# Graph convolution on one core: twelve products of zeros added to every group's open sum of messages

## The chip, the cores and the metric

The kernel runs on one core of one Trainium2 chip. The metric is device time in microseconds (us) of one execution; three runs give a median. The engines are named as the profile names them: PE (TensorE, matrix products, with PEld for its weight loads), DVE (VectorE), ACT (ScalarE), POOL (GpSimd, which here issues the gathers) and SP (SyncE, which issues the other DMAs).

## The reference, cut to what matters

Two graph layers run one after the other over 6250 nodes and 200000 edges that are sorted by destination. The first is a two-layer attention network, the second a convolution with radial weights. The change touches only the convolution:

```python
e0, e1 = f0[edge_src], f1[edge_src]                       # 128 numbers per edge, gathered
h = gelu(gelu(edge_scalar_attr @ W_mlp1 * c1) @ W_mlp2 * c2)
w = einsum('pxu,ex->epu', W_tp, h)                        # 4 x 32 weights per edge
mid = concatenate([w0*e0*a0, w3*(e1.a1), w1*e0*a1, w2*e1*a0])   # 256 numbers per edge
agg = zeros.at[edge_dst].add(mid)                         # sum of messages per node
out = mix of agg @ Wf0, agg @ Wf1 and the node's own part
```

## The kernel before, in words

**Tiles, groups, chunks.** The edges are cut into 1563 tiles of 128, one edge per partition. Eight tiles make a group (196 groups), and three groups, 24 tiles (`CT`), make a chunk. A chunk's messages are added into one sum `whole` in PSUM, 128 node slots by 256 columns, of which there is a single buffer. A Python loop over groups writes the program out in full; `keep` holds the instructions of each engine in the order in which the loop writes them, so that each engine is a queue whose first instruction blocks those behind it.

**One group on each engine.**
- POOL issues eight gathers, one per tile, into a tile `G` (line 353). There are six `G` buffers; a gather waits until ACT and DVE have read the buffer's old contents.
- ACT runs two gelus (`hid`, line 1479), eight scalings of the gathered rows (`g`, line 1495), and in some groups a copy.
- PE runs the two layers of the small network (line 1476: `layer<-a8t` with 16 rows, then `layer<-hid`), eight products for the weights (`big`, line 1488), and eight products that add the messages into the sum (`whole<-mess,ohr`, line 1531). These are fp32, and each stands in the trace as two records.
- DVE multiplies out the messages (lines 1508 to 1517) and makes the next group's one-hot matrix (`ohr`, line 1524).
- SP issues the loads of `a8t` (line 1595) and of what a chunk's end needs.

**The order on PE** decides much below. In all groups it begins with `layer<-a8t` for a later group. In a chunk's first group the eight weight products, `layer<-hid` and the eight message products follow; the first of these opens the new sum, so it needs ACT's copy of the old one (`acc<-whole`, line 1561, in `close`), which stands on ACT between the two `hid`. After six of the eight, two products at line 1579 carry the old sum's shared nodes over. In the second group `layer<-a8t` is followed by the transposes of the old sum (line 1539); in the third, by the chunk's last products (lines 1544 and 1545), whose result ACT copies at line 1547 (`o`). After these come `layer<-hid`, the weight products and the message products, as before.

The first message product of a chunk starts the sum (`k == 0`), and the last one closes it (`k == end` in `sink`).

Of the kernel before, what the change touches and what calls it, by code (L numbers as in the profile page):

```python
# [32 lines left out]
BF16 = mybir.dt.bfloat16  # L33
# [10 lines left out]
P = 128  # L44
# [4 lines left out]
WSTEP = 16  # L49
HS = 7  # L50
CT, LT = 24, 40
DENSE1 = 24
LAG_D, AFTER, AFTER_D = 11, 4, 7
GP, GK, GSB = 125, 16, 4
# [10 lines left out]
def gnn_kernel(ctx: ExitStack, tc: tile.TileContext, x, src, dst, attr4, attr8,  # L65
# [3 lines left out]
    nc = tc.nc  # L69
    N, D = x.shape  # L70
# [23 lines left out]
    NT = src_t.shape[1]  # L94
    NG = NB - DENSE1
    HALF = P // 2
# [16 lines left out]
    keep = tc.keep_in_program_order  # L113

    def big():
        return ps_big.tile([P, 8, P], F32, tag="big", name="big")
# [10 lines left out]
    def whole():  # L127
        return ps_acc.tile([P, 512], F32, tag="acc", name="whole")
# [392 lines left out]
    def flags(pool, *why):  # L521

        flag = pool.tile([1, NB + 1], F32, name="flag")
        nc.vector.tensor_copy(flag[:, :NB], why[0])
        for w in why[1:]:
            nc.vector.tensor_tensor(flag[:, :NB], flag[:, :NB], w, op=OP.max)
        nc.vector.tensor_reduce(flag[:, NB:], flag[:, :NB], axis=AX.X, op=OP.max)
        flag_i = pool.tile([1, NB + 1], I32, name="flag_i")
        nc.vector.tensor_copy(flag_i, flag)
        return flag_i[:, :NB], flag_i[:, NB:]  # L530
# [146 lines left out]
    keep = lambda ins: ins  # L677
# [78 lines left out]
    rhs1 = [dram.tile([P, NB, HW], BF16, name=f"rhs1{q}") for q in range(H1 // 2)]  # L756
    deg1 = pool.tile([P, DENSE1], F32, name="deg1")

# [185 lines left out]
    def miscounted(pool, deg, edges, n):  # L944


        many = pool.tile([P, n], F32, name=f"many{n}")
        nc.vector.tensor_scalar(many, deg, 256.0, None, op0=OP.is_gt)
        ps = small()
        nc.tensor.matmul(ps[:1, :n], ones, deg, start=True, stop=True)  # L950
        nc.tensor.matmul(ps[:1, P:P + n], ones, many, start=True, stop=True)
        miss = pool.tile([1, n], F32, name=f"miss{n}")
        nc.vector.tensor_tensor(miss, ps[:1, :n], edges, op=OP.subtract)
        nc.vector.tensor_tensor(miss, miss, ps[:1, P:P + n], op=OP.subtract)
        nc.vector.tensor_scalar(miss, miss, -0.5, None, op0=OP.is_lt)
        return miss

    HH = H1 // 2 * C1
    assert DENSE1 % 4 == 0
    passes = [(b0, q) for b0 in range(NG, NB, 4) for q in range(H1 // 2)]  # L960
# [173 lines left out]
    def chunk_of(g):  # L1134
        return (g * SB + HT // 2) // HT

    def first_of(c):
        return max(0, HT * c - HT // 2)

    def last_of(c):  # L1140
        return HT * c + HT // 2
# [13 lines left out]
    def scatter(g, tiles):  # L1155
        c = chunk_of(g)
        if tiles[0] == 0 and g * SB == first_of(c):
            kept1["acc"] = whole()[:, :HD + H1]
        for t in tiles:
            nc.tensor.matmul(kept1["acc"], ohs[g][:, t, :], mss[g][:, t],  # L1160
                             start=g * SB + t == first_of(c), stop=g * SB + t + 1 == last_of(c))
# [85 lines left out]
    keep = plain  # L1247
    nc.vector.tensor_scalar(wtp_sb[:, 0:3, :], wtp_sb[:, 0:3, :], 1.0 / math.sqrt(HID), None, op0=OP.mult)
    nc.vector.tensor_scalar(wtp_sb[:, 3, :], wtp_sb[:, 3, :], 1.0 / math.sqrt(3.0 * HID), None, op0=OP.mult)
    written_order.close()  # L1250
    nc.vector.tensor_tensor(over1[:, NG:], over1[:, NG:], miscounted(pool, deg1, n_edges[:, NG:], DENSE1), op=OP.max)
    again, some = flags(pool, over1, wide1.to_broadcast([1, NB]))
# [58 lines left out]
    with tc.tile_pool(name="att2", bufs=1) as pool, tc.tile_pool(name="dense", bufs=2) as dense, \  # L1311
# [68 lines left out]
        for b0 in range(0, NB, 2):  # L1380
            n = min(2, NB - b0)
# [10 lines left out]
            acc = big().rearrange("p (k a) c -> p k (a c)", k=2)  # L1392
            if b0 == 8:
                load_tiles(pool)
            for h0 in range(0, NB, HS):
# [15 lines left out]
                for j, made in ((0, up), (1, down)):  # L1411
                    for h in range(HS):
                        for k in range(n):
                            nc.tensor.matmul(acc[:, k, j * C2:(j + 1) * C2], made[:, h, k * P:(k + 1) * P],
                                             rhs2[:, h0 + h, j, :],
                                             start=h0 + h + j == 0, stop=h0 + h + j == NB)
# [3 lines left out]
            acc = acc[:, :n, :2 * C2].rearrange("p k (j c) -> p k j c", j=2)  # L1420
# [30 lines left out]
    cw = ctx.enter_context(tc.tile_pool(name="cw", bufs=2))  # L1451
# [46 lines left out]
    def messages(G, g0, n, a1, pw, then, between):  # L1498


        w = pw[:, :n, :].rearrange("e c (p u) -> e c p u", p=4)
        ms = cw.tile([P, SB, 2, 4, MUL], F32, name="mess", bufs=3)
        e0 = G[:, :n, :MUL]
        e1 = G[:, :n, MUL:].rearrange("e c (i u) -> e c i u", i=3)
        s4 = [P, n, 3, MUL]

        dot = cw.tile([P, SB, 3, MUL], F32, name="dot", bufs=1)
        keep(nc.vector.tensor_tensor(dot[:, :n], e1, a1[:, :, :, None].to_broadcast(s4), op=OP.mult))  # L1508
        dot1 = cw.tile([P, SB, MUL], F32, name="dot1", bufs=1)
        keep(nc.vector.tensor_reduce(dot1[:, :n], dot[:, :n].rearrange("e c i u -> e c u i"), axis=AX.X, op=OP.add))  # L1510
        w1 = cw.tile([P, SB, MUL], F32, name="w1", bufs=1)
        keep(nc.vector.tensor_tensor(w1[:, :n], w[:, :, 1, :], e0, op=OP.mult))  # L1512
        keep(nc.vector.tensor_tensor(ms[:, :n, 1, 0], w[:, :, 3, :], dot1[:, :n], op=OP.mult))
        keep(nc.vector.tensor_tensor(ms[:, :n, 1, 1:], w[:, :, 2, :][:, :, None, :].to_broadcast(s4),
                                     g0[:, :n, MUL:].rearrange("e c (i u) -> e c i u", i=3), op=OP.mult))
        keep(nc.vector.tensor_tensor(ms[:, :n, 0, 0], w[:, :, 0, :], g0[:, :n, :MUL], op=OP.mult))  # L1516
        keep(nc.vector.tensor_tensor(ms[:, :n, 0, 1:], w1[:, :n, None, :].to_broadcast(s4),  # L1517
                                     a1[:, :, :, None].to_broadcast(s4), op=OP.mult))
        between()
        got = then and then()  # L1520
        return ms, got

    def one_hot3(dl, n, oh):
        keep(nc.vector.tensor_tensor(oh[:, :n, :], slot[:, None, :].to_broadcast([P, n, P]),  # L1524
                          dl[:, :, None].to_broadcast([P, n, P]), op=OP.is_equal))
        return oh

    def scatter(ms, oh, cs, sink):
        for c in cs:
            acc, start, stop = sink(c)  # L1530
            keep(nc.tensor.matmul(acc, oh[:, c, :], ms[:, c].rearrange("e h i u -> e (h i u)"), start=start, stop=stop))  # L1531
# [19 lines left out]
    with tc.tile_pool(name="conv", bufs=1) as pool, tc.tile_pool(name="gath3", bufs=6) as gath:  # L1551
# [4 lines left out]
        state, todo = {}, deque()  # L1556
# [12 lines left out]
        def sink(t):  # L1569
            c, k = divmod(t, CT)  # L1570
            end = min(CT, NT - c * CT) - 1
            if k == 0:
                state["acc"] = whole()[:, :2 * D]
            if k == min(6, end) and c:

                same = cw.tile([P, P], F32, name="same")
                keep(nc.vector.tensor_scalar(same, slot, shift[:, c - 1:c], None, op0=OP.is_equal))
                for a in state["sums"]:
                    keep(nc.tensor.matmul(state["acc"], same, a, start=False, stop=False))  # L1579
            return state["acc"], k == 0, k == end  # L1580

        groups = [(t, min(SB, NT - t)) for t in range(0, NT, SB)]

        def hots(g):
            t, n = groups[g]
            return one_hot3(dstc[:, t:t + n], n, cw.tile([P, SB, P], F32, name="ohr", bufs=3))

        def layers(g):
            if g >= len(groups):
                return iter(())  # L1590
            t, n = groups[g]
            a8t = cw.tile([2 * NRAD, NPR * P], F32, name="a8t", bufs=4)
            for j in range(2 if n > NPR else 1):
                c = (t + j * NPR) * P
                nc.sync.dma_start(a8t[j * NRAD:(j + 1) * NRAD, :], attr8_t[:, c:c + NPR * P])
            return hidden(n, a8t)
# [8 lines left out]
        def keep_a1(t):  # L1605
            m = min(LT, NT - t)
            a1s = kept[:, P + t // LT % 2 * 3 * LT:P + (t // LT % 2 + 1) * 3 * LT].rearrange("p (k f) -> p k f", f=3)
            keep(nc.vector.tensor_copy(a1s[:, :m], a4s[t][:, :m, 1:]))
            return a1s
# [21 lines left out]
        for g, (t, n) in enumerate(groups):  # L1631
            G, g0 = rows
            i = t % LT
            last = g + 1 == len(groups)
            ms, after = messages(G, g0, n, a1s[:, i:i + n, :], pws.popleft(), None if last else lambda: hots(g + 1),
                                 lambda: hids.extend(list(second)[-1:]))
            if i + SB == LT and t + SB < NT:
                a1s = keep_a1(t + SB)
            first = layers(g + 3)
            next(first, None)  # L1640
            if not last:
                rows = fetch(g + 1)
            next(first, None)
            pw = big() if hids or todo else None
            if todo:
                todo.popleft().send(pw)
                next(first, None)
            if t and t % CT == 0:
                close(t // CT - 1)
            if hids:  # L1650
                pws.append(weigh(groups[g + 2][1], hids.popleft(), pw))
            next(first, None)
            scatter(ms, oh, range(n), lambda c: sink(t + c))
            second = first
            oh = after
# [117 lines left out]
```

## Time and profile before

| What | Value |
|---|---|
| median of 3 runs | 4942.67 us (4939.53 to 4945.52) |
| profiled execution | 4904.63 us, span 4902.8 us |
| mean granted PE clock | 0.796 of full speed |
| convolution, 2400 to 4800 us of the span: PE, DVE, ACT, POOL busy | 1599.58, 1105.17, 684.29, 1374.04 us |
| the same stretch: granted PE clock, share of DMA engines | 0.78, 0.18 |

The span is the time from the first to the last instruction of one profiled execution. Busy time is the union of an engine's instructions. A row of the timeline gives start, length, engine, line, operation, tiles, shapes and count; in brackets stands how long the engine was idle before and what ended that. "remote" means that a semaphore did so and that the profile found no instruction that ended just then.

### The profile page before, as it was taken

The page shows a single profiled execution, that of the slowest core. Times are in us where ns is not written, and L with a number is a line of the kernel's source. Part 1 is how long each engine was busy: PE and PEld are TensorE (multiplying, and loading weights), DVE is VectorE, ACT ScalarE, POOL GpSimd, SP SyncE. Part 2 cuts the span into 40 slices and gives each one's busy share as a digit, 9 for nine tenths or more (in the row PEclk, how much of TensorE's full clock was granted, in tenths as well). Part 3 has the DMA queues.
Part 4 walks back from the last instruction along what each step waited for, and adds up shares of the span by engine and source line. Part 5 has one row for each costly group of instructions (what it writes and reads, how often), then busy time and mean ns, then how long its engine had stood idle before and what let it go on. Part 6 is the DMA issues. An engine that isn't in the chain of part 4 may idle for free.

```text
span 4902.8 us, 63767 instructions
## 1 busy us (share of the span) xinstructions
PE 3315.7 (68%) x21302; PEld 2434.5 (50%) x21303; DVE 2951.3 (60%) x4901; ACT 2432.3 (50%) x5811; POOL 2488.7 (51%) x2440
## 2 busy tenths in 40 slices
PE   3247777777667789995466766666666675666667
PEld 3145555555445578884244444444444443444445
DVE  5458778788778779995344444444444444444445
ACT  3238878888678679995223322222222232222233
POOL 4556666667556500002555555555555555555553
PEclk6558878889788789997677877777777877777788
DMA  3346666667566554442111111111111111111111
GB/s 100 91 119 180 176 173 178 176 184 198 155 166 185 165 217 158 166 171 74 46 45 48 48 48 47 47 48 47 47 49 47 47 49 47 46 48 48 47 46 30
DMA packets 420348, 491.23 MB, mean 100 GB/s; under 512 B 267937, under 2 KB 303628, under 8 KB 419998
## 3 DMA queue, kind: packets, MB, share of 16 engines
q1 hardware_dynamic: 340900, 345.68, 23.4%
q0 software_dynamic: 78304, 139.36, 11.8%
q8 instruction: 175, 2.87, 0.2%
q10 hardware_dynamic: 794, 1.88, 0.1%
q14 instruction: 175, 1.43, 0.1%
HBM read 383.20 MB, written 103.42 MB: 99 GB/s over the span
## 4 chain that ended last, share of the span: by engine, by line
another core or an unknown queue 21%; PE 19%; ACT 6%; issue 5%; DVE 2%; DMA 0%; DVEq 0%; ACTq 0%; SPq 0%
PE whole L1531 9%; PE layer L1476 6%; ACT g L1495 4%; PE big L1488 3%; ACT hid L1479 1%; DVE mess L1517 1%; PE whole L1579 0%; PE big L1544 0%; DVE ohr L1524 0%; DVE dot L1508 0%; DVE mess L1516 0%; DMA G<-table,srcc 0%; DVE dot L1510 0%; PE big L1539 0%
## 5 line engine op out<-in xcount | busy, mean ns | idle before, releaser
L353 POOL DMA_INDIRECT G<-table,srcc x1563 | 1475.1, 944 | 1622.4 <-ACT g L1495 571.8
L353 POOL DMA_INDIRECT G<-table,srcw x808 | 955.1, 1182 | 616.9 <-DVE msg L394 294.4
L1479 ACT ACTIVATE hid<-layer 128x512 f32<-128x512 f32 x392 | 233.5, 596 | 1605.2 <-remote 963.2
L1531 PE MATMUL whole<-mess,ohr 128*128 128x256 f32 x3126 | 819.4, 417 | 0.5 <-ACT acc L1561 0.5
L1096 ACT ACTIVATE up<-erb,sel 128x512 bf16<-128x512 f32 x1176 | 809.3, 739 | 0.4 <-PE small L878 0.4
L1476 PE MATMUL layer<-hid,wm_sb 128*128 128x512 f32 x392 | 301.4, 860 | 676.8 <-ACT hid L1479 464.9
L1531 PEld LDWEIGHTS whole<-mess,ohr 128*128 128x128 f32 x3126 | 649.9, 212 | 157.1 <-issue 53.3
L878 PE MATMUL small<-key,lo 128*128 128x98 bf16 x3136 | 315.0, 232 | 387.9 <-ACT ca L860 165.4
L860 ACT CAST ca<-small 128x392 bf16<-128x392 f32 x784 | 385.7, 495 | 291.2 <-remote 135.6
L878 PEld LDWEIGHTS <-lo 128*128 128x128 bf16 x3136 | 285.0, 123 | 478.3 <-issue 447.5
L1524 DVE TENSOR_TENSOR ohr<-kept,dstc 128x1024 f32<-128x1024 f32 x196 | 238.6, 1218 | 470.4 <-remote 337.7
L1512 DVE TENSOR_TENSOR w<-big,G 128x256 f32<-128x256 f32 x196 | 82.5, 421 | 696.4 <-PE big L1488 308.8
L1011 PE MATMUL up<-up,rc 128*102 128x512 bf16 x1176 | 475.3, 437 | 37.8 <-DVE up L1020 11.7
L1495 ACT ACTIVATE g<-G,a 128x128 f32<-128x128 f32 x1563 | 475.4, 390 | 0.0
L1401 ACT ACTIVATE ramp<-erb,sel 128x256 bf16<-128x256 f32 (+1 forms) x1138 | 458.0, 493 | 13.4 <-DVE up L1409 7.5
L1488 PEld LDWEIGHTS big<-wtp_sb,hid 64*128 64x128 f32 x3126 | 258.3, 246 | 386.0 <-ACT o L1547 211.0
L1476 PEld LDWEIGHTS layer<-hid,wm_sb 128*128 128x128 f32 x392 | 74.1, 237 | 714.4 <-ACT hid L1479 487.0
L1488 PE MATMUL big<-wtp_sb,hid 64*128 64x128 f32 x3126 | 303.7, 349 | 180.8 <-ACT o L1547 151.1
L1020 DVE TENSOR_TENSOR up<-up,ctc 128x3584 bf16<-128x3584 bf16 x168 | 339.4, 2020 | 55.1 <-ACT up L1096 26.5
L1160 PEld LDWEIGHTS whole<-msg,ohr 128*128 128x128 f32 x1616 | 329.5, 242 | 61.7 <-issue 21.2
L852 DVE TENSOR_TENSOR lo<-slots,turned 128x2048 bf16<-128x2048 bf16 x196 | 238.5, 1217 | 155.2 <-PE small L878 87.5
L1160 PE MATMUL whole<-msg,ohr 128*128 128x68 f32 x1616 | 322.6, 315 | 0.7 <-ACT ring L1166 0.7
(316 smaller groups left out, 5100.3 us busy)
## 6 DMA issues: line engine op xcount, KB each, us to landing
counts<-ca SPq DMA_DIRECT2D x196, 392.0 KB
ct<-counts SPq DMA_DIRECT2D x196, 392.0 KB
ctc<-counts SPq DMA_DIRECT2D x1344, 56.0 KB
rc<-rhs SPq DMA_DIRECT2D x84, 358.8 KB
oht<-dlow SPq DMA_DIRECT2D x50, 512.0 KB
G<-table,srcc POOLq DMA_INDIRECT x1563
G<-table,srcw POOLq DMA_INDIRECT x808
a8t<-attr_rows SPq DMA_DIRECT2D x391, 16.0 KB
```

The costliest lines, as they stand in the source:

```text
L353: nc.gpsimd.indirect_dma_start(out=G[:, c, :], out_offset=None, in_=table, in_offset=bass.IndirectOffsetOnAxis(ap=idx[:, c:c + 1], axis=0))
L860: nc.scalar.copy(ca[:, :, k * W:(k + WBANK) * W].rearrange("p h (k d) -> p h k d", d=W), ps[:, :WBANK * NKEY].rearrange("p (k h d) -> p h ...
L878: nc.tensor.matmul(ps[:, n * NKEY:(n + 1) * NKEY], lo[:, a, :, r], ky[:, a, :, r], start=True, stop=True)
L1011: nc.tensor.matmul(sums["ups"][j][:2 * C1, :], r[:, i, c:c + 2 * C1], up[:, i], start=h0 + i == 0, stop=h0 + i == NB - 1)
L1020: nc.vector.tensor_tensor(by_part, by_part, state["ct", p, h0].rearrange("p k a h d -> p h (k a) d"), op=OP.min)
L1096: nc.scalar.activation(up[:, i], state["erb", p][:, j], AF.Relu, bias=sel1[:, h0 + i, 2 * q + j:2 * q + j + 1], scale=STEEP)
L1160: nc.tensor.matmul(kept1["acc"], ohs[g][:, t, :], mss[g][:, t], start=g * SB + t == first_of(c), stop=g * SB + t + 1 == last_of(c))
L1401: nc.scalar.activation(ramp[:, h, :n * P], erb[:, :n * P], AF.Relu, bias=sel2[:, h0 + h, :], scale=STEEP)
L1476: keep(nc.tensor.matmul(ph, w, x[:, :npr * P], start=True, stop=True))
L1488: keep(nc.tensor.matmul(pw[:, c, :], hid[half, j * P:(j + 1) * P], wtp_sb[half].rearrange("x p u -> x (p u)"), start=True, stop=True))
L1495: keep(nc.scalar.activation(g0[:, c], G[:, c, :], AF.Copy, scale=a0[:, c, :]))
L1531: keep(nc.tensor.matmul(acc, oh[:, c, :], ms[:, c].rearrange("e h i u -> e (h i u)"), start=start, stop=stop))
```

## The change

A tile of 128 by 128 bf16 zeros is made once. In every group but the first, right after `layer<-a8t` on PE, twelve products of this tile with 256 columns of zeros (one column, read 256 times) are added into the sum `whole` that is then open. In a chunk's first group this is still the old chunk's sum, and the last of the twelve closes it; the message products no longer do, save the very last. The values of the sum stay what they were.

```diff
+BUSY = 12
...
+    nothing = cw.tile([P, P], BF16, name="nothing", bufs=1)
+    nc.vector.memset(nothing, 0.0)
+
+    def busy(acc, n, stop):
+
+        for i in range(n):
+            keep(nc.tensor.matmul(acc, nothing, nothing[:, 0:1].to_broadcast([P, 2 * D]),
+                                  start=False, stop=stop and i == n - 1))
+
...
-            return state["acc"], k == 0, k == end
+            return state["acc"], k == 0, t + 1 == NT
...
             next(first, None)
+            if t:
+                busy(state["acc"], BUSY, t % CT == 0)
             pw = big() if hids or todo else None
```

In the built program this is 2340 products, each with a weight load of its own (195 groups times 12), and one memset on DVE. All other instructions stand in their old order on every engine. One wait is new: ACT's copy `acc<-whole` now waits for the last of the twelve products before it; before the change its data were known to be there from the wait of the `hid` ahead of it.

## The prediction

> **What bounds the kernel now.** I read the page first, for the stages.
>
> ```profile
> PE 3315.7 (68%) x21302; PEld 2434.5 (50%) x21303; DVE 2951.3 (60%) x4901; ACT 2432.3 (50%) x5811; POOL 2488.7 (51%) x2440
> ...
> POOL 4556666667556500002555555555555555555553
> PEclk6558878889788789997677877777777877777788
> ...
> L353 POOL DMA_INDIRECT G<-table,srcc x1563 | 1475.1, 944 | 1622.4 <-ACT g L1495 571.8
> ```
>
> No engine is full. From slice 20 on, the convolution, POOL is busy five tenths and the granted clock is 0.7 to 0.8. The busy times by stretch and the waits of line 353 tell more (the second is "idle until: us, times").
>
> ```profile
> 2400.00:4800.00 2400.00, 1599.58 (x7268) 1071.81 (x7267) 1105.17 (x1549) 684.29 (x2002) 1374.04 (x1456) 0.78 0.18 47
> ```
>
> ```profile
>   ACT g L1495: 548.6, 98
> ```
>
> In these 2400 us POOL issues 1456 gathers, so 182 groups, so a chunk of three groups takes 2400 / (182 / 3) = 39.6 us. A gather costs 0.944 us and 0.30 us of issue; 24 of them make 29.9 us. The other 9.7 us of a chunk POOL stands idle, nearly always for ACT's `g`. So the chunk lasts as long as POOL's gathers plus POOL's waits, and the question is what makes ACT late. The timeline of one chunk shows it.
>
> ```profile
> 3056.01 1.12 PE L1476 MATMUL layer<-a8t,wm_sb 16*128 16x512 f32 x2
> ...
> 3065.69 0.60 ACT L1479 ACTIVATE hid<-layer 128x512 f32<-128x512 f32 x1 [11.39 <-remote]
> 3066.34 2.08 PE L1476 MATMUL layer<-hid,wm_sb 128*128 128x512 f32 x2 [8.34 <-issue]
> 3068.67 0.94 POOL L353 DMA_INDIRECT G<-table,srcc  x1 [0.30 <-issue]
> 3072.75 0.27 ACT L1547 COPY o<-big 128x128 f32<-128x128 f32 x1 [6.47 <-remote]
> 3073.40 2.44 ACT L1495 ACTIVATE g<-G,a 128x128 f32<-128x128 f32 x8
> 3076.36 0.94 POOL L353 DMA_INDIRECT G<-table,srcc  x1 [6.75 <-ACT g L1495]
> 3080.60 1.12 PE L1476 MATMUL layer<-a8t,wm_sb 16*128 16x512 f32 x2
> 3081.82 0.60 ACT L1479 ACTIVATE hid<-layer 128x512 f32<-128x512 f32 x1 [5.97 <-issue]
> 3082.31 0.37 ACT L1561 COPY acc<-whole 128x256 f32<-128x256 f32 x1
> 3082.74 1.12 PE L1476 MATMUL layer<-hid,wm_sb 128*128 128x512 f32 x2
> 3087.70 0.60 ACT L1479 ACTIVATE hid<-layer 128x512 f32<-128x512 f32 x1 [5.03 <-remote]
> 3090.90 0.94 POOL L353 DMA_INDIRECT G<-table,srcc  x1 [4.86 <-ACT g L1495]
> 3091.16 1.13 PE L1476 MATMUL layer<-hid,wm_sb 128*128 128x512 f32 x2 [1.72 <-ACT hid L1479]
> 3092.33 0.60 ACT L1479 ACTIVATE hid<-layer 128x512 f32<-128x512 f32 x1 [0.96 <-PE layer L1476]
> ```
>
> Compare the end of a product with the start of the ACT instruction that reads it. At 3092.29 and 3092.33 they are 0.04 us apart; POOL has then been gathering for 1.4 us. But the product that ends at 3057.13 is read at 3065.69, 8.6 us late, and the one that ends at 3083.86 at 3087.70, 3.8 us late: POOL has then been gathering for 15.7 and 11.3 us. The copy `o` at 3072.75, whose product was recorded before 3058.1, comes 3.1 us after the last gather's end. So while gathers run on for over about five us, PE's work reaches its readers late, and it all arrives some 2 to 3 us after the gathers stop. Why, the trace does not say. The cycle is: 16 gathers (19.7 us), late reports, `hid` and `g` on ACT, a POOL wait of 6.75; 8 gathers (9.7 us), late reports, `hid` and `g`, a POOL wait of 4.86. PE's speed is off this path so long as its work is done before the late report.
>
> **The change, part by part.**
>
> *The memset.* One in DVE's queue before the loop, hidden by DVE's 1295 idle us in that stretch; at worst below 1 us.
>
> *The products' own time.* The nearest row is bf16 with 196 columns in the attention stage, at a clock of 1.0.
>
> ```profile
> 2100.58 1.34 PE L1414 MATMUL big<-rhs,down 128*128 128x196 bf16 x14
> ```
>
> Fourteen in 1.34 us, of which the last one's own length (0.25, the mean of that line) is drained: 1.09 / 13 = 84 ns from start to start, with the weight loads beside. For 256 columns that is 110 ns, for twelve 1.32 us, for 195 groups 257 us. At half the clock it would be 514 us, but `layer<-a8t` just before lasts 1.12 us here, as at full clock. Where do the 1.32 us go? In a chunk's third group (3057.13) PE stands idle 8.3 us afterwards: hidden. In its second group PE waits 1.72 us for `hid` at 3091.16: hidden. In its first group PE goes on at once, and nothing covers them; but `layer<-hid` would end at 3085.2 instead of 3083.86 and is read only at 3087.70. So I take 0 here; if the cover were gone the price is 65 x 1.32 = 86 us for the first groups and 257 us for all.
>
> *Closing the sum with a product of zeros.* This moves the flag and costs no time, but it makes the new wait: ACT's `acc<-whole` (3082.31) waits for the report of the twelfth product. On ACT the second `hid` and eight `g` queue behind it, and for those POOL; on PE the message products of the first group wait for the copy. The twelve end at about 3083.0. If the report is prompt the copy moves by 0.7 us and still precedes `layer<-hid`'s end: cost 0. If it is as late as that of `layer<-hid` (3087.70), the copy moves by 5.4 us. The nearest row is the latter, recorded one us later in the same queue. I take a copy about 3 us later. Then: (a) the copy's 0.37 us falls between the late report and `hid`, so up to 0.37 us on POOL's wait of 4.86. (b) The first group's message products start 2 to 2.5 us later (they start 0.96 us after the copy now), the next `layer<-a8t` too. There ACT's `hid` had 1.7 us of slack (3088.8 to 3090.53), but PE now also runs twelve products before line 1539, so `layer<-hid` moves from 3091.16 to about 3093. (c) So the third group's `layer<-a8t` falls some 2 us deeper into the 16 gathers, where reports are later. Today it is mostly read before the gathers end (3065.69 against 3069.61), so that ACT's `hid` and PE's `layer<-hid` (0.6 + 2.08 us) still run within them. Read only at the end, they come on top: POOL's wait grows from 6.75 us by up to 2.7. I take 1.4, half. With 65 closings: 65 x (0.37 + 1.4) = 115 us; bounds 0 and 65 x (0.37 + 2.7) = 200 us.
>
> *More records before each report.* 24 more instructions per group pass PE's queue, 30% more than the 80 records (7268 + 7267 over 182 groups). If a late report depends on how many there are, the delays grow, with the bound just given. If it depends on time alone, 0.
>
> *The clock.* Between 3065 and 3069 a `layer<-hid` takes 2.08 us, at 3082 1.12: half the clock after the long idle stretch. The products fill 1.32 of those 8 us, so the drop stays. In the second group they fill the 1.72 us, and a drop after it (the message products at 3093.96 take 4.69 us, at 3052.36 3.72) may go: 1 us, off the path. The Trainium skill ("TensorE: Matmul & The Clock Gate", HAM oscillation) says that idle gaps of PE above about 3.4 us drop the clock to half, and names continuous work as the remedy. The row agrees that the long gap does; by the page 1.32 us in it leave the drop, and if the drop went anyway the sum would lose the 110 us that the faster rival names.
>
> The sum: 115 us. The profiled execution is 4904.63 us, its span 4902.8; it lies 38 us below the median, and I carry that difference over: a profile after should show about 5020. On the median: 4942.67 + 115 = 5058 us.
>
> **The rivals.**
> - *All of it hides.* Reports of the twelfth product are prompt; POOL's gathers and late reports set the pace alone. For: idle PE after two of three groups. Against: the late reports just shown. About 4943 us.
> - *The clock rises, and it is faster.* Over 2400 us the clock is 0.78, and one drop less per chunk, 3.4 us at half speed, would save 1.7 us in the chain after a POOL wait, 65 x 1.7 = 110 us: 4833 us. It decides if the drop after the third group's idle time goes, or if prompt products shorten reports. Against: 1.32 us are a sixth of that gap, and zeros may not count as work.
> - *PE becomes the bound.* Nothing covers the products: +257 us, 5200 us. Against: 800 idle us of PE in the stretch.
> - *The sixteen gathers split.* If `layer<-hid` in the second group moves past the first five us of gathers, its report is late, `g` waits, and POOL gets a third wait per chunk of about 4 us: 65 x 4 + 115, about 5320 us. `layer<-hid` ends 1.4 us into the gathers now and has some 3 us to spare.
>
> **How the numbers follow.** Forecast (slower, 4970 to 5150) 0.46; hidden 0.12; faster 0.22; PE the bound 0.12; split 0.08. A change below 0.2%, 10 us, can't be told from none here. Faster 0.22, same 0.12, slower 0.66. The range leaves out the split and the deeper half of the faster case, and takes in the PE bound: 4870 to 5210; the likeliest case alone 4970 to 5150.
>
> **What would show it.** Right: `acc<-whole` starts some 3 us or more after the `hid` ahead of it, with "remote" or a line of zeros as its release; the 65 POOL waits after 16 gathers grow from 6.75 towards 9; the clock stays near 0.78. Wrong: the clock in the convolution near 1.0 and the 8 us gaps gone; or `acc<-whole` within 1 us and POOL's idle time unchanged; or POOL waits after every eight gathers.

## The result, and the profile after

The changed kernel takes 5016.28 us (median of 4 runs, 5007.62 to 5027.9), the kernel before 4941.10 us beside it (4 runs, 4932.71 to 4945.52): a ratio of 1.0156, 95% interval 1.0129 to 1.0183, or 75 us more. The profiled execution is 5027.9 us, its span 5025.8.

One thing is needed to read all that follows. The kernel before is not equally long at all times: it took 4941 us here, 4771 and 4753 us beside two of the experiments, and 3977 to 3981 us beside the others, on one and the same chip 3977, 4753 and 3980 us. So each experiment is compared only with the kernel before that ran beside it. I call the two conditions *late* and *prompt*, after what the profile shows below.

First the page after: its first part, the slices and the line of the gathers.

```profile
PE 3523.3 (70%) x23642; PEld 2618.6 (52%) x23643; DVE 2951.6 (59%) x4902; ACT 2435.4 (48%) x5811; POOL 2491.9 (50%) x2440
...
PEclk7558888888888699996788888888888888888889
...
L354 POOL DMA_INDIRECT G<-table,srcc x1563 | 1474.5, 943 | 1728.9 <-ACT g L1496 679.7
```

PE is 208 us busier. POOL's gathers (now line 354) last as long as before, but their wait for ACT's `g` has grown from 571.8 to 679.7 us, by 108 us, of the 123 us by which the two profiled executions differ: the loss is there. By stretch of time, the same columns as before:

```profile
2400.00:4800.00 2400.00, 1717.44 (x9133) 1190.76 (x9131) 1066.21 (x1497) 663.29 (x1931) 1321.42 (x1401) 0.83 0.18 46
```

In 2400 us POOL now issues 1401 gathers instead of 1456, so a chunk lasts 2400 / (1401 / 24) = 41.1 us instead of 39.6. PE does more in it and stands idle less, and the granted clock is 0.83 instead of 0.78. The timeline of one chunk after:

```profile
3107.93 0.60 ACT L1480 ACTIVATE hid<-layer 128x512 f32<-128x512 f32 x1 [12.86 <-remote]
3108.58 2.07 PE L1477 MATMUL layer<-hid,wm_sb 128*128 128x512 f32 x2 [8.57 <-ACT hid L1480]
...
3117.32 0.95 POOL L354 DMA_INDIRECT G<-table,srcc  x1 [6.96 <-ACT g L1496]
...
3121.30 1.50 PE L1535 MATMUL whole<-nothing 128*128 128x256 bf16 x12
...
3123.01 0.37 ACT L1571 COPY acc<-whole 128x256 f32<-128x256 f32 x1 [0.96 <-PE whole L1535]
...
3123.82 1.12 PE L1477 MATMUL layer<-hid,wm_sb 128*128 128x512 f32 x2
...
3128.84 0.60 ACT L1480 ACTIVATE hid<-layer 128x512 f32<-128x512 f32 x1 [5.45 <-PE whole L1541]
...
3132.03 0.94 POOL L354 DMA_INDIRECT G<-table,srcc  x1 [5.03 <-ACT g L1496]
```

The cycle has stayed: long gathers, late `hid`, `g`, a wait of POOL, twice a chunk. The copy `acc` does wait for the twelfth product now, 0.96 us here. But look at the first group, whose gathers begin at 3117.32: `layer<-hid` ends at 3124.94, 7.6 us later, and is read at 3128.84, after they have ended.

A count over the trace's rows of line 354 sums this up. Runs of gathers with 0.30 us between them are taken as one burst, and the idle time after a burst is POOL's wait less those 0.30 us. "Through" means an idle time under 4 us, a wait cut short. The few bursts of other lengths are left out of the first columns, not of the last.

| Trace | bursts of 8: number, mean idle after, through | bursts of 16: the same | POOL idle between bursts |
|---|---|---|---|
| before (4904.63 us) | 55, 3.33 us, 36 | 64, 6.18 us, 6 | 605 us |
| after (5027.9 us) | 74, 3.99 us, 27 | 55, 7.16 us, 0 | 713 us |

The chunk of the kernel before that the prediction shows has a burst of eight that is not through (4.86 us). This is a first group of that kernel which is:

```profile
3469.19 0.94 POOL L353 DMA_INDIRECT G<-table,srcc  x1 [7.00 <-ACT g L1495]
...
3473.73 1.12 PE L1476 MATMUL layer<-hid,wm_sb 128*128 128x512 f32 x2
...
3477.72 0.60 ACT L1479 ACTIVATE hid<-layer 128x512 f32<-128x512 f32 x1 [4.05 <-remote]
...
3480.91 0.94 POOL L353 DMA_INDIRECT G<-table,srcc  x1 [2.04 <-ACT g L1495]
```

`layer<-hid` ends at 3474.85, 5.7 us after the burst's first gather, and is read at 3477.72, before the last gather ends (3478.87). POOL then stands idle for 2.04 us, 1.74 us by the count.

### The profile page after: what moved, and what is told of

Same layout as the page of the kernel before. It is cut to its first block, busy times and chain, and to the rows that moved or that the text cites. A ratio compares the mean times of both kernels' runs of the same rounds, so it can differ in the third digit from the quotient of the medians.

```text
span 5025.8 us, 68446 instructions
## 1 busy us (share of the span) xinstructions
PE 3523.3 (70%) x23642; PEld 2618.6 (52%) x23643; DVE 2951.6 (59%) x4902; ACT 2435.4 (48%) x5811; POOL 2491.9 (50%) x2440
## 3 DMA queue, kind: packets, MB, share of 16 engines
q14 instruction: 175, 1.43, 0.1%
## 4 chain that ended last, share of the span: by engine, by line
PE 22%; another core or an unknown queue 21%; ACT 5%; issue 4%; DVE 1%; POOL 0%; DMA 0%; DVEq 0%; ACTq 0%
PE whole L1541 10%; PE layer L1477 5%; ACT g L1496 4%; PE big L1489 4%; PE whole L1535 3%; ACT hid L1480 1%; DVE mess L1518 0%; PE whole L1589 0%; PE big L1549 0%; ACT acc L1571 0%; PE big L1554 0%; DVE mess L1517 0%; ACT o L1557 0%; POOL G L354 0%
## 5 line engine op out<-in xcount | busy, mean ns | idle before, releaser
L354 POOL DMA_INDIRECT G<-table,srcc x1563 | 1474.5, 943 | 1728.9 <-ACT g L1496 679.7
L1477 PE MATMUL layer<-hid,wm_sb 128*128 128x512 f32 x392 | 267.7, 771 | 439.8 <-ACT hid L1480 298.1
L1489 PEld LDWEIGHTS big<-wtp_sb,hid 64*128 64x128 f32 x3126 | 244.7, 223 | 473.1 <-ACT o L1557 241.0
```

The lines of the kernel that those rows point to most:

```text
L354: nc.gpsimd.indirect_dma_start(out=G[:, c, :], out_offset=None, in_=table, in_offset=bass.IndirectOffsetOnAxis(ap=idx[:, c:c + 1], axis=0))
L1477: keep(nc.tensor.matmul(ph, w, x[:, :npr * P], start=True, stop=True))
L1489: keep(nc.tensor.matmul(pw[:, c, :], hid[half, j * P:(j + 1) * P], wtp_sb[half].rearrange("x p u -> x (p u)"), start=True, stop=True))
```

## The experiments

My theory was that of the prediction: ACT's new wait, of the copy for the twelfth product, is what costs. The rivals: 24 more PE instructions in a group make every report later; or PE's own time for them isn't hidden.

**Where the kernel before takes 3980 us, nothing costs.** The first four kernels ran beside a kernel before of 3977.44 us. The first takes the new wait out and leaves the products; the first groups' twelve go to the buffer of the weight products, and `busy` gets a fourth argument, `start`, which opens that buffer:

```diff
-            if t:
-                busy(state["acc"], BUSY, t % CT == 0)
+            if t and t % CT:
+                busy(state["acc"], BUSY, False)
             pw = big() if hids or todo else None
+            if t % CT == 0 and pw is not None and t:
+                busy(pw[:, 0:2, :].rearrange("p c u -> p (c u)"), BUSY, True, True)
...
-            return state["acc"], k == 0, t + 1 == NT
+            return state["acc"], k == 0, k == end
```

> All 2340 products of zeros but twelve stay where they are, but the one new wait is taken out: in a chunk's first group the twelve are written into the buffer that the weight products overwrite right after, and the last message product closes the sum again, so ACT's copy of the sum waits for nothing new. My theory (the wait of the copy for the twelfth product is what costs) expects nearly the time before, 4941 to 4960 us, with the copy again within 0.1 us of the gelu ahead of it and POOL idle between its gathers for about 605 us. The rival that 24 more PE records in every group make every report later expects it to stay at the changed kernel's 5000 to 5030 us; the rival that the products' own time is not covered in the first groups expects the same.

The second keeps only the wait, with one product:

```diff
-            if t:
-                busy(state["acc"], BUSY, t % CT == 0)
+            if t and t % CT == 0:
+                busy(state["acc"], 1, True)
```

> Only the wait: a single product of zeros in each chunk's first group, which closes the sum, and none in the other groups. My theory expects most of the loss, 4985 to 5015 us, since the copy still waits for a product that stands after the first layer product; it is less than the changed kernel's only by the eleven products' 1.3 us before the report. The rivals (number of records, products' own time) expect the time before, 4941 us within 10.

The third is the second with `BUSY`, twelve, in place of 1.

> The twelve products and the moved close in each chunk's first group alone, none in the other two. My theory expects the whole loss, 5005 to 5025 us. If the number of records counts beside the wait, it lies between the single product's time and the changed kernel's, with a third of the records' part; if the records alone count, about 4941 + 75 / 3 = 4966 us.

The fourth is the first with `BUSY = 24`.

> 24 products in every group and no new wait (the first groups' go into the buffer that the weight products overwrite, and the message products close the sum). My theory expects no more than a few us above the time before, 4941 to 4970 us, as PE still has idle time; the clock may rise above the 0.83 of the changed kernel. If the number of records sets the delay of reports, it expects twice the loss, 5090 us; if the products' own time is uncovered in the first groups, 65 x 2.6 = 170 us more, 5110 us.

Measured: 3980.17, 3978.14, 3980.69 and 3978.04 us, ratios 1.0006 (0.9995 to 1.0016), 1.0000 (0.9989 to 1.0010), 1.0009 (0.9999 to 1.0019) and 1.0002 (0.9993 to 1.0011). No expectation was met where it named a loss, and the four don't tell the theories apart, since the loss itself is missing. (In this condition no kernel with up to twelve products a group, nor the one with 24, differs by more than 0.12%.) Then the changed kernel itself, beside a kernel before of 3980.74 us:

> The changed kernel itself, unaltered, beside the kernel before on one chip. In the first four runs the kernel before took 3977 us instead of 4941, its POOL gathered without a pause and PE's results were read at once, so nothing that the changed kernel adds can be late there. My theory (the copy's new wait costs only where PE's results are reported late while gathers run) expects: if the kernel before takes about 3977 us here, the changed kernel takes the same within 0.2%; if it takes about 4940 us, the changed kernel takes some 75 us more. A rival that the products cost by themselves expects more time in both cases.

It took 3985.25 us, 1.0008 (0.9997 to 1.0019). So the first half of that expectation holds. What is different is seen in its list of waits, from 2400 to 3600 us ("engine line <- awaited: us in total, times, longest"):

```profile
ACT g L1496 <- DMA G<-table,srcc: 552.9, 671, 2.4
...
POOL G L354 <- issue: 258.1, 847, 0.3
...
ACT hid L1480 <- PE layer L1477: 118.2, 120, 1.9
```

and in its timeline:

```profile
3013.28 0.36 ACT L1571 COPY acc<-whole 128x256 f32<-128x256 f32 x1
3013.43 1.12 PE L1477 MATMUL layer<-hid,wm_sb 128*128 128x512 f32 x2 [0.65 <-ACT hid L1480]
...
3014.60 0.60 ACT L1480 ACTIVATE hid<-layer 128x512 f32<-128x512 f32 x1 [0.95 <-PE layer L1477]
```

POOL no longer waits for ACT (its list has one such wait, of 0.3 us, the pause that lies before every gather): its 1563 gathers follow one another at 1.248 us on the mean from the first to the last, and ACT waits for the gathers' data instead. `layer<-hid` ends at 3014.55 and is read at 3014.60, 0.05 us later, though gathers are running without a pause; in that stretch no `hid` waits over 1.9 us for its product, where the late kernel before had waits of up to 17.8 us for a "remote" release (its list, 2400 to 4800 us):

```profile
ACT hid L1479 <- remote: 854.5, 103, 17.8
```

In the prompt condition PE's results are read at once, the chunk is 24 x 1.248 = 30.0 us of gathers, and the products lie beside them.

Two repeats of the first kernel were meant for the case of a late condition, and met a prompt one both times:

> The products of zeros without the new wait, as in the first of the earlier runs, now beside the changed kernel on the same chip. If the kernel before takes about 4940 us here: by my theory 4941 to 4960 us, since the copy no longer waits; by the rival that the number of records sets the delay, 5000 to 5030 us. If it takes about 3977 us: the same time within 0.2%.

> The products without the new wait once more, for the case that the kernel before takes about 4940 us here, with PE's results read late while gathers run: then my theory (the copy's wait) expects 4941 to 4960 us, and the rival that the number of PE records or the products' own time costs expects 5000 to 5030 us. If the kernel before takes about 3980 us, as on the two chips so far: 3980 us within 0.2%, and nothing new is learnt.

They took 3984.92 us, 1.0005 (0.9995 to 1.0016), and 3982.60 us beside 3980.47, 1.0012 (1.0002 to 1.0022).

**How many products fit.** The fourth kernel with `BUSY = 36`:

> 36 products in every group without the new wait. Where gathers run without a pause (the kernel before at 3977 us) a chunk lasts 30 us; PE needs about 25.5 us of it with one product at a clock of 0.88, about 23 us at full clock, and 108 products of 110 ns add 11.9 us. So PE should become the bound, 35 us a chunk, about 5 x 65 = 325 us more, 4300 us; POOL should then wait in every group. Where the kernel before takes 4940 us: if only the wait counts and PE's idle time covers the rest, at most 65 first groups x 4 us = 260 us more; if the number of records sets the delay, well over 5200 us.

It took 4230.24 us beside 3980.74, 1.0619 (1.0601 to 1.0638): 250 us more, where 325 were expected. The stretches of the kernel with 24 products (2200 to 3800 us) and of this one (2400 to 3600 us):

```profile
2200.00:3800.00 1600.00, 1598.50 (x10256) 1173.81 (x10253) 959.59 (x1367) 691.03 (x1763) 1209.32 (x1282) 1.00 0.24 63
```

```profile
2400.00:3600.00 1200.00, 1200.00 (x8088) 902.58 (x8086) 648.17 (x908) 408.26 (x1175) 814.46 (x863) 1.00 0.22 57
```

With 24 products PE is busy 1598.5 of 1600 us and POOL still issues a gather every 1.248 us: PE is all but full, and the products cost nothing. With 36 PE is busy all the time and POOL issues 863 in 1200 us, one every 1.39 us: PE is the bound.

The next kernel is the third with `BUSY = 36`: 36 products in the first groups alone, and the copy waits for the last.

> 36 products and the close in each chunk's first group alone, none elsewhere: as many products as three groups of twelve, but the last one, for which the copy waits, comes about 2.6 us later than in the changed kernel. Where the kernel before takes about 3980 us, POOL's gathers set the pace (30 us a chunk), PE needs about 23 us of it at full clock and 65 x 36 products add 4 us a chunk: no change within 0.3%, although the copy now waits some 2 to 3 us after the gelu ahead of it. Where the kernel before takes about 4940 us: by my theory more than the changed kernel's 75 us, up to 65 x (1.2 + 2.6) = 250 us; by the rival that only the number of products counts, the same 75 us.

It took 3983.23 us beside 3980.47, 1.0007 (0.9998 to 1.0017), as expected, though the copy waits:

```profile
3020.13 4.17 PE L1535 MATMUL whole<-nothing 128*128 128x256 bf16 x36
...
3024.34 0.37 ACT L1571 COPY acc<-whole 128x256 f32<-128x256 f32 x1 [1.00 <-PE whole L1535]
```

The copy starts 0.04 us after the last product's end: the wait is real, the report prompt, and POOL's lead hides it. The first row also gives the price of a product: less the last one's own length of 0.27 us, (4.17 - 0.27) / 35 = 111 ns from start to start.

**Where PE's results are late, the products cost without the wait.** This kernel closes the sum with a product of zeros ahead of `layer<-a8t`, so that the wait of the first `hid` covers the copy; the first groups' twelve go to the buffer of the weight products, as above.

```diff
             first = layers(g + 3)
+            if t and t % CT == 0:
+                busy(state["acc"], 1, True)
             next(first, None)
```

> The sum is closed by a product of zeros, as in the changed kernel, but by a single one that stands ahead of the first group's first layer product, so that the gelu's wait ahead of ACT's copy covers it; the twelve of that group go into the buffer that the weight products overwrite. All else as in the changed kernel. Where the kernel before takes about 4940 us: by my theory (the wait for a product behind the layer product costs) at most 10 us over the time before; by the rival that the number of records or the products' own time costs, 5000 to 5030 us. Where it takes about 3980 us: the same within 0.2%.

The kernel before took 4771.43 us beside it, this one 4940.08 us: 1.0356 (1.0312 to 1.0400), 169 us more. That is the late condition, and my theory falls there: the wait is gone, the loss isn't. Its waits from 2400 to 4800 us, and a first group in its timeline:

```profile
ACT hid L1480 <- remote: 738.2, 103, 16.7
POOL G L354 <- ACT g L1496: 676.2, 117, 7.6
```

```profile
3131.92 0.94 POOL L354 DMA_INDIRECT G<-table,srcc  x1 [6.73 <-ACT g L1496]
...
3136.93 1.50 PE L1535 MATMUL big<-nothing 128*128 128x256 bf16 x12
...
3137.59 0.37 ACT L1571 COPY acc<-whole 128x256 f32<-128x256 f32 x1
...
3139.46 1.13 PE L1477 MATMUL layer<-hid,wm_sb 128*128 128x512 f32 x2
...
3140.65 0.94 POOL L354 DMA_INDIRECT G<-table,srcc  x1 [0.30 <-issue]
...
3143.27 0.60 ACT L1480 ACTIVATE hid<-layer 128x512 f32<-128x512 f32 x1 [5.32 <-remote]
```

The copy follows the first `hid` at once (over all 66 copies ACT stands idle 0.08 us before it on the mean, as in the kernel before). The twelve products lie between 3136.93 and 3138.43, `layer<-hid` ends at 3140.59, 8.7 us after the burst's first gather, and is read 1.7 us after its last (3141.59). ACT stood idle for 5.32 us before it. All 61 bursts of eight of this trace end alike: the idle time after them is 4.60 us with a standard deviation of 0.04, and none is through.

Then the wait alone, the second kernel once more:

> The wait alone, as in the second of the earlier runs: one product of zeros closes the sum in each chunk's first group, and ACT's copy waits for it. In the last run, on a chip where the kernel before took 4771 us, the products without this wait cost 169 us, so my theory that the wait is the cause has fallen for that chip; open is whether the wait costs anything beside them. Where the kernel before takes over 4700 us: if the wait counts too, 20 to 115 us more; if the products ahead of the layer product are the whole cause, within 20 us of the kernel before. Where it takes about 3980 us: the same within 0.2%.

Beside a kernel before of 4753.32 us, late again, it took 4761.82 us: 1.0017 (0.9992 to 1.0042), 8 us more and not to be told from none. The copy does wait for this one product, but hardly: 0.20 us on the mean. POOL's waits for `g` (its list, 2400 to 4400 us) are no longer than in the one trace of the kernel before:

```profile
ACT hid L1480 <- remote: 616.3, 89, 23.7
...
POOL G L354 <- ACT g L1496: 364.9, 69, 8.9
```

That is 364.9 / 69 = 5.3 us each, against 548.6 / 98 = 5.6 there. The same count of bursts for these two traces:

| Trace | bursts of 8: number, mean idle after, through | bursts of 16: the same | POOL idle between bursts |
|---|---|---|---|
| wait alone (4750.8 us) | 43, 3.12 us, 33 | 71, 5.39 us, 19 | 533 us |
| products, no wait (4949.67 us) | 61, 4.60 us, 0 | 63, 6.39 us, 0 | 695 us |

The two kernels differ by 162 us of POOL's idle time, and the kernels before beside them by only 18 us. The products take away the early reports, and the wait for one product does not.

The rows of the first groups alone show how. For each burst of eight in which (or in the pause after which) a first group's `layer<-hid` ends, take the time from the burst's first gather to that end:

| Trace | such bursts | `layer<-a8t` to `layer<-hid`, end to end, median | end of `layer<-hid` in the burst, median | through, of those that end under 7 us | through, of those above |
|---|---|---|---|---|---|
| before | 40 | 2.15 us | 6.50 us | 24 of 26 | 2 of 14 |
| wait alone | 27 | 2.36 us | 7.07 us | 12 of 13 | 6 of 14 |
| after | 42 | 3.58 us | 7.92 us | 1 of 2 | 0 of 40 |
| products, no wait | 60 | 3.58 us | 8.46 us | 0 of 0 | 0 of 60 |

Twelve products push `layer<-hid` back by 1.43 us, past the place up to which it is mostly read early, and the bursts of first groups that are through fall from 26 of 40 to 1 of 42, with the copy's wait or without it. The kernel before, with no instruction added, rarely gets through beyond that place either, so the delay in time is enough to account for most of the early reports lost. That it is all isn't shown: with the wait alone, on another occasion, 6 of 14 still get through there.

Last, small products, which should have told the number of instructions from PE's time:

```diff
-            keep(nc.tensor.matmul(acc, nothing, nothing[:, 0:1].to_broadcast([P, 2 * D]),
-                                  start=False, stop=stop and i == n - 1))
+            keep(nc.tensor.matmul(acc[:8, 0:8], nothing[:, 0:8], nothing[:, 0:8],
+                                  start=start and i == 0, stop=stop and i == n - 1))
```

> As many products as in the changed kernel (twelve in every group but the first) and no new wait, but small ones: 8 by 8 numbers instead of 128 by 256, so that they need a fraction of the 1.5 us that twelve took, while the number of PE's instructions ahead of each awaited product is the same; those of the first groups go into the buffer that the weight products overwrite, and the message products close the sum. Where the kernel before takes over 4700 us (PE's results are read late while gathers run): if the number of instructions ahead of a report sets its delay, some 100 to 170 us more, as with full products; if PE's time ahead of it counts, in proportion to their length, at most 60 us more. The time alone can't tell the two apart if it falls between. Where the kernel before takes about 3980 us: the same within 0.2%.

It met the prompt condition: 3980.59 us beside 3979.50, 1.0008 (0.9999 to 1.0017). So it doesn't tell the two apart.

## Why the prediction was right or wrong, point by point

- **The sum.** 115 us were forecast, 75 measured; 5058 against 5016.28 us. A profile of about 5020 was named, and it is 5027.9. Sign and size hold, and POOL's waits for `g` are where the loss lies, as forecast. But the term that carried the sum, the wait of `acc<-whole`, is not what costs where it could be tested; a term that was put at 0 is. That the time fell into the forecast range is therefore largely luck.
- **The new wait, (a) to (c), 115 us: the step that failed.** With one product it is worth 8 us (interval -4 to 20). It was charged at "a copy about 3 us later", between a prompt report (0.7) and one as late as that of `layer<-hid` (5.4); after the change ACT stands idle 1.70 us before the copy on the mean of all 66, before 0.08. The loss is there without that wait: 169 us where the copy waits for nothing new. What the wait for the *twelfth* product adds in the late condition to the products' own effect stays open: the wait was tried there with one product only.
- **The products' own time.** 110 ns a product was right (111 measured); twelve take 1.50 us and not 1.32, since the last one's own length was left out. "In its first group ... I take 0 here" was wrong in the late condition. The cover was read from one chunk, in which `layer<-hid` was read only after the gathers anyway. The trace of before has such chunks and others: in 26 of the 40 bursts of eight with a first group's `layer<-hid`, POOL waited under 4 us. The products push that `layer<-hid` back by 1.43 us, and of the early ones 1 of 42 is left after the change and 0 of 60 without the wait. The 169 us lie between the bounds given, 86 us if the first groups aren't covered and 257 us if none is, but by chance: those priced PE's own time, and what is lost is the early report.
- **More records before each report, taken as 0.** Its bound was named, but no share of it went into the forecast. The place in time of `layer<-hid` accounts for most of what the traces show; that the number of instructions adds nothing was not settled, as the kernel that should tell them apart ran where nothing is late.
- **The late reports.** "Over about five us" of gathers is borne out by the counts below. "It all arrives some 2 to 3 us after the gathers stop" is too coarse: many results are read before the gathers end, as in the prediction's own row at 3065.69. And at 3087.70 POOL had not "been gathering" for 11.3 us: its eight gathers had ended at about 3086.
- **(c), POOL's wait after 16 gathers.** Forecast from 6.75 to about 9 us in all chunks; it is 7.16 us on the mean against 6.18, and 74 bursts of eight instead of 55. The sign is right, and the size is about half. That the copy's wait makes it, as the chain of (a) to (c) has it, isn't shown: without the new wait it is 6.39 us, on another occasion.
- **The clock.** It rose to 0.83, where "near 0.78" was said; the drop after the third group's gap stayed (`layer<-hid` at 3108.58 still takes 2.07 us). How long a drop lasts, the 3.4 us of the faster rival, no run here shows.
- **The rivals.** "All of it hides" is what happens in the prompt condition. "PE becomes the bound" needs more than 24 products there. "The sixteen gathers split" came in part: 55 bursts of 16 instead of 64 and 19 more of eight, where a third wait in every chunk was priced. "Faster by the clock" never came: even a clock of 1.00 moves nothing when POOL's gathers set the pace. The Trainium skill ("TensorE: Matmul & The Clock Gate", HAM oscillation) names continuous work of PE as the remedy for a dropped clock. The 24 products agree with it (clock 1.00, against 0.89 with one product a chunk), and they also show that the remedy buys no time where PE isn't the bound (3978.04 us beside 3977.44).

Why this loss is 75 us beside a kernel before of 4941 us and 169 us, for the kernel without the wait, beside one of 4771 us, was only argued: POOL's idle time with the products is about the same, 713 and 695 us, so the kernel before that got more reports through early would have had more to lose. No trace of the kernel before at 4771 us was taken.

## What to carry to other kernels

An engine's idle time isn't free to fill: what stands ahead of a result that another engine awaits delays it, and if that result has a deadline (here, coming through before the gathers hold it up), a small delay costs the whole wait. Read the cover of an added instruction over all repetitions, not from one chunk, and look at the spread of the waits. And run the kernel before beside each experiment: the changed kernel lost 75 us in one condition and nothing that could be told from none in the other.

## What the runs showed of the hardware that was not expected

- The same kernel on the same chip took 3977, 4753 and 3980 us at different times. The gathers last 0.94 us in both conditions; what differs is how soon the reader of a product starts after the product's recorded end: 0.05 us in the prompt one, 8.6 us in the chunk that the prediction showed. Which circumstance outside the kernel makes the condition, no run shows.
- In the four late traces together, ACT stood idle for over 1 us after the recorded end of a `layer` product in 7 of the 467 cases where that end lay less than 5 us after the first gather of a burst of 8 or 16, and in 428 of 568 where it lay 7 us or more after it, the gathers still running. Why, no trace says.
- Products of zeros raise the granted clock. From 2400 to 3600 us, all in the prompt condition, the granted clock is 0.89 with one product a chunk, 0.98 with twelve a group and 1.00 with 24; with twelve small ones of 8 by 8 it is 0.89.
- A product of 128 by 128 with 256 columns that are one column read again takes 111 ns from start to start; the record of one lasts 272 ns at the median.
